# Residuals of four attention layers held by tokens, and planned tiles in place of rings, in a two-layer network on one Trainium2 core

## The chip, the cores and the metric

The kernel runs on one core of a Trainium2 chip. The core has five engines that run at the same time and wait for each other by semaphores: TensorE (PE: matmuls and transposes, results into PSUM), VectorE (DVE), ScalarE (ACT), GpSimd (POOL) and SyncE (SP, which issues DMAs here). PSUM is divided into 8 tiles of 128 x 512 floats in this kernel; POOL works on SBUF alone here. The metric is the device time in microseconds (us) of one execution. The median of three runs before the change is 562.79 us (561.96 to 564.04).

## What is computed

The input is 2048 tokens of 128 features (8 sequences of 256). Two layers follow, each with an attention part and a feed-forward part, and a normalisation `(x - mean) / sqrt(var + eps)` after each residual sum.

- First layer: a simple attention, a router, and for each token the two best of 8 expert networks.
- Second layer: two grouped convolutions over the tokens, then four layers of linear attention, a feed-forward part of width 512, and a second one with four weight matrices of width 512.

The change concerns the second layer's attention. Cut to what matters:

```
h = layernorm(conv2(gelu(conv1(x))) + x, ln0_g, ln0_b)
for i in range(4):
    q, k = gelu(h @ Wq[i] + bq[i]) + 0.21, gelu(h @ Wk[i] + bk[i]) + 0.21
    v = h @ Wv[i] + bv[i]
    z  = 1 / (q . mean(k) + 1e-6)          # per head and token
    kv = rope(k)^T v / n
    out = rope(q) kv * z
    h = layernorm(out + h, lnA_g[i], lnA_b[i])   # (t - mean) / sqrt(var) * g + b
f = gelu(h @ W1 + b1) @ W2 + b2
h = layernorm(f + h, ln2_g, ln2_b)
```

The residual of each layer, the `h` in `out + h`, is thus a normalised tile times a factor plus a shift per feature.

## The kernel before

The first layer ends near 185 us with the experts' results scattered to DRAM (`ys`). For the second layer the tokens are cut into 4 blocks of 512 (`blk`, two sequences each). `second_layer(blk)` doesn't issue instructions at once. It adds steps to a plan (`Steps.add`, by way of `do`), each with its engine, a cost in ns, the tiles it reads and writes and the new tiles it takes. `Steps.order` then makes one order for all engines by list scheduling: among the steps that could start first, with those up to 50 ns later, it picks the one with the highest rank (length of the longest chain behind it) plus a bias of its block, 3000 * (NB - blk) ns. Each engine's instructions are issued in that order and run in order on the chip, so a waiting instruction holds up all behind it on its engine. `Steps.trace` issues them.

A new tile comes from a ring: 8 PSUM tiles (`ps`), 21 tiles of 128 x 512 (`tmp`), 5 wide ones (`hid`), 7 of `featT`, 2 of `got`, 4 each of `xp` and `kvh`. A ring hands out its buffers in turn, so a step waits until the oldest one has been read for the last time.

The steps of a block, with the lines of the profile:

- SP fetches the experts' results (`got`, L882). DVE adds both to the residual, four sub-tiles with two instructions each, in one step (L890, L891), takes the moments (L823, L825), POOL makes the root (L343, and a power at L344), DVE centres and scales (L846), PE transposes (L868), ACT copies into the padded tile (L915).
- Convolutions: 20 matmuls each (L921, L938) with four GELUs between (L930), the sum (L944), transposes back to tokens, moments, root, centring into `n0`, transposes to features, and on ACT the factor and shift into `h0` (L954).
- One attention layer, with `h` by features: PE makes k (L970), q (L981) and v (L993); ACT the GELUs (L977, L982, L986); PE transposes k (L1015). DVE multiplies by the rope tables: for k from PSUM (L1018, L1024), for q from SBUF (L1035, L1033), and POOL adds the two halves (L1030 for k, L1037 for q). PE forms k^T v (L1044), DVE masks it by heads (L1050); PE forms the denominators (L1058, L1062) from means (L1005) and DVE inverts them (L1072, L1073); PE forms the numerators (L1079), DVE multiplies them by z (L1085).
- The residual: PE transposes `h` back to tokens (`back`, L1092) into a PSUM tile `pr`, and DVE adds it to the result `s` (L1095).
- The norm of the layer: DVE takes moments of `s`, POOL makes root and shift (L343, L344, L836, L837), ACT scales and shifts `s` in place (L857), PE transposes it (L868), ACT applies the layer's factor and shift by features into the next `h` (L954).
- The feed-forward parts: L1109 and L1120, then L1153, L1173 (two wide products) and L1194, the last block's in two halves; the result goes to DRAM (L1207).

The lines of the residual before:

```
def back():
    for i in range(NT):
        nc.tensor.transpose(t("pr")[:, i * P : (i + 1) * P], T(hT)[:, i * P : (i + 1) * P], ident)

do_("PE", 600, back, f"{hT} s", pr="ps")
do_("DVE", 680, lambda: nc.vector.tensor_add(t("s"), t("pr"), t("s")), "pr", "s")
```

Of the kernel before, what the change touches and what calls it, by code (L numbers as in the profile page):

```python
# [10 lines left out]
F32 = mybir.dt.float32  # L11
# [57 lines left out]
    ("bv", L * D), ("ln2_g", D), ("ln2_b", D),  # L69
# [63 lines left out]
class Steps:  # L133
# [19 lines left out]
    def order(self):  # L153
# [10 lines left out]
        over, taken, free = {}, {ring: [] for ring in self.rings}, {}  # L164
        ready, found = [i for i in range(n) if not missing[i]], []
        while ready:
            starts = {}
            for i in ready:
                engine, cost, _, needs, new, _, bias = self.steps[i]
                t = free.get(engine, 0)  # L170
                for d in needs:
                    on, lag = self.steps[d][0], self.steps[d][5]
                    t = max(t, end[d] + lag + (self.HOP.get(on, 80) if on != engine else 0))
                for name, ring in new.items():
                    at = len(taken[ring]) - self.rings[ring][0]
                    if at >= 0:
                        t = float("inf") if left[taken[ring][at]] else max(t, over[taken[ring][at]])
                if t < float("inf"):
                    starts.setdefault(engine, []).append((t, i))
            if not starts:  # L180
                raise AssertionError([(self.steps[i][0], self.steps[i][4], {r: [(x, left[x]) for x in taken[r][-self.rings[r][0]:]] for r in self.steps[i][4].values()}) for i in ready])
            first = min(min(s)[0] for s in starts.values())
            t, i = max(
                ((t, i) for s in starts.values() if min(s)[0] == first for t, i in s if t <= first + 50),
# [6 lines left out]
            for name, ring in new.items():  # L191
                taken[ring].append(name)
# [11 lines left out]
    def trace(self):  # L204
        for i in self.order():
            _, _, run, _, new, _, _ = self.steps[i]
            for name, ring in new.items():
                self.tiles[name] = self.rings[ring][1]()
            run()
# [3 lines left out]
def tile_network(ctx: ExitStack, tc: tile.TileContext, a: dict, out: bass.AP):  # L213
# [558 lines left out]
    tmpp = ctx.enter_context(tc.tile_pool(name="tmp1", bufs=21))  # L772
    pairp = ctx.enter_context(tc.tile_pool(name="pairs", bufs=2))
# [12 lines left out]
    def chunked(ap):  # L786
# [6 lines left out]

    plan = Steps({
        "ps": (8, ps), "tmp": (21, tmp), "hid": (5, hidden), "featT": (7, featT),
        "got": (2, lambda: pairp.tile([P, NT, K, D], F32, tag="got", name="got")),
        "xp": (4, lambda: tmpp.tile([P, BB, PADN], F32, tag="xp", name="xp", bufs=4)),
        "kvh": (4, lambda: tmpp.tile([P, BB, D], F32, tag="kvh", name="kvh", bufs=4)),
# [3 lines left out]
    def second_layer(blk):  # L802
# [3 lines left out]
        def do(engine, cost, run, reads="", writes="", lag=0, behind="", **new):  # L806
            plan.add(
                engine, cost, run, of(reads), of(writes) + of(" ".join(new)),
                {f"{n}.{blk}": ring for n, ring in new.items()}, lag, 3000 * (NB - blk), of(behind),
            )  # L810
# [7 lines left out]
        def moments_of(src, mv, n=NT, at=0, cost=1240):  # L818
# [9 lines left out]
            do("DVE", cost * n // NT, run, src, mv)  # L828
# [13 lines left out]
        def centre(dst, src, mv, r, n=NT, at=0, cost=1120, **new):  # L842
# [8 lines left out]
            do("DVE", cost * n // NT, run, f"{src} {mv} {r}", "" if dst in new else dst, **new)  # L851
# [12 lines left out]
        def turn(dst, src, n=NT, at=0):  # L864

            def run():
                for i in range(at, at + n):
                    nc.tensor.transpose(T(dst)[:, i * P : (i + 1) * P], T(src)[:, i * P : (i + 1) * P], ident)  # L868

            do("PE", 590 * n // NT, run, src, **{dst: "ps"})  # L870
# [8 lines left out]
        def fetch():  # L879
            for k in range(K):  # L880
                at = k * B * N + blk * TB
                nc.sync.dma_start(out=T("got")[:, :, k, :], in_=ys[at : at + TB, :].rearrange("(i p) d -> p i d", p=P))  # L882

        do("SP", 1200, fetch, lag=1800, got="got")

        def combine():
            for i in range(NT):
                n = blk * NT + i
                s, x = by_tile(T("s"))[:, i, :], xs[blk][:, i, :]
                nc.vector.scalar_tensor_tensor(s, T("got")[:, i, 0, :], m1[:, n : n + 1], x, ALU.mult, ALU.add)  # L890
                nc.vector.scalar_tensor_tensor(s, T("got")[:, i, 1, :], m2[:, n : n + 1], s, ALU.mult, ALU.add)  # L891

        do("DVE", 2300, combine, "got", s="tmp")
        if blk == 0:

            do("ACT", 1500, lambda: nc.scalar.activation(
                small.tile([P, 1], F32, tag="warm", name="warm"), T("s")[:, 0:1], AF.Gelu), "s", "")
        moments_of("s", "mvc")
        root_of("mvc", "rc", 1e-5)

        def own():
            keep_as("x", res().rearrange("p i d -> p (i d)"))

        do("DVE", 0, own, "", "x")
        centre("x", "s", "mvc", "rc")
        turn("px", "x")


        def padded():
            for t in (T("xp"), T("h1").rearrange("p (g b n) -> p g b n", g=NG, b=BB)):  # L910
                nc.vector.memset(t[..., 0:2], 0.0)
                nc.vector.memset(t[..., N + 2 : N + 4], 0.0)

        do("DVE", 200, padded, xp="xp", h1="hid")
        do("ACT", 600, lambda: nc.scalar.copy(T("xp")[:, :, 2 : N + 2], by_batch(T("px"))), "px", "xp")  # L915

        def conv1():
            for k in range(KW):
                for g in range(NG):
                    at = slice(g * CG, (g + 1) * CG)  # L920
                    nc.tensor.matmul(  # L921
                        T(f"pg{g}"), lhsT=taps1[at, k, :], rhs=T("xp")[at, :, k : k + N],
                        start=(k == 0), stop=(k == KW - 1), tile_position=(g * CG, 0),
                    )

        do("PE", 4600, conv1, "xp", **{f"pg{g}": "ps" for g in range(NG)})
        for g in range(NG):
            def gelu1(g=g):
                h1 = T("h1").rearrange("p (g b n) -> p g b n", g=NG, b=BB)
                nc.scalar.activation(h1[:, g, :, 2 : N + 2], by_batch(T(f"pg{g}")), AF.Gelu, bias=col("conv1_b", g))  # L930

            do("ACT", 640, gelu1, f"pg{g} h1", f"hg{g}")

        def conv2():
            h1 = T("h1").rearrange("p (g b n) -> p g b n", g=NG, b=BB)
# [7 lines left out]
        do("PE", 5900, conv2, "h1 hg0 hg1 hg2 hg3", pc="ps")  # L943
# [15 lines left out]
        def attention(l, hT, out):  # L959
# [130 lines left out]
            def back():  # L1090
                for i in range(NT):
                    nc.tensor.transpose(t("pr")[:, i * P : (i + 1) * P], T(hT)[:, i * P : (i + 1) * P], ident)  # L1092

            do_("PE", 600, back, f"{hT} s", pr="ps")
            do_("DVE", 680, lambda: nc.vector.tensor_add(t("s"), t("pr"), t("s")), "pr", "s")  # L1095
# [12 lines left out]
        for c in range(FC):  # L1108
# [9 lines left out]
            by_tile(T("xb")), by_tile(T("x")), row("ln2_b").unsqueeze(1).to_broadcast([P, NT, D])), f"x {hT}", xb="tmp")  # L1118
# [100 lines left out]
def _laid_out(v):  # L1219
# [6 lines left out]
    def by_group(x):  # L1226
# [24 lines left out]
        "ln2_g": v["L1_attn_ln2_g"], "ln2_b": v["L1_attn_ln2_b"],  # L1251
    }
# [38 lines left out]
```

## Time and profile before

| what | value |
|---|---|
| median of three runs | 562.79 us |
| the profiled execution's own time | 559.73 us |
| its span, first to last instruction | 558.0 us |
| mean granted TensorE clock | 0.935 |
| first layer's last result written to DRAM | 187.3 us |
| first transpose of the second layer (L868) | 197.4 us |
| first product of an attention layer (L970) | 242.2 us |
| first L1109 (feed-forward) | 358.9 us |
| last product of an attention layer (L1079) | about 366 us |
| end of the last L1194 | 547.4 us |
| transposes back, L1092 | 64, 9.7 us busy |

The profile records one execution. "Busy" is the time in which an engine had at least one instruction under way; since instructions overlap in an engine's pipeline, and matmuls above all, a mean duration is longer than the distance from one start to the next. A group's line gives line, engine, operation, output and input tiles, shapes and count, then busy us and mean ns of one, then the idle time of the engine just before them and what ended it. A window's line gives the stretch and its length, then busy us and number of instructions of PE, PEld (weight loads), DVE, ACT and POOL, then the granted clock, the DMA share and GB/s. A wait's line gives who waited for whom, us in all, times, and the longest. fp32 matmuls count as two passes, transposes as one.

### The profile page before, as it was taken

Reading aid. Unit: us, or ns where it says so; the run is one execution under the profiler, and the core shown is the slowest. Engines: PE = TensorE matmul, PEld = TensorE weight load, DVE = VectorE, ACT = ScalarE, POOL = GpSimd, SP = SyncE. Lnnn points to the kernel's source line nnn. Section 1 sums busy time; section 2 is a strip of 40 time slices with the busy share of each in tenths; the row PEclk is TensorE's granted clock in tenths of the full one; section 3 lists DMA queues with packets and bytes.
Section 4 is the critical chain, followed back from the end, with each engine's and each line's share of the span. In section 5 each row is a group of like instructions: output and inputs, shape, how many; then the busy total and the mean of one; then the engine's idle time right before and its main releaser. Section 6 shows DMA issues by size and latency. Waiting matters only on the chain.

```text
span 558.0 us, 7642 instructions
## 1 busy us (share of the span) xinstructions
PE 494.5 (89%) x2557; PEld 332.5 (60%) x2557; DVE 299.7 (54%) x1009; ACT 221.6 (40%) x478; POOL 202.0 (36%) x275
## 2 busy tenths in 40 slices
PE   5875289999999079999999899999999999999992
PEld 3655179999999033467787778754444444444442
DVE  1996524444444491379999999938943020022232
ACT  4561044444444123163958676654322120312110
POOL 1860375777643220035565555644200000000011
PEclk9965569999999679999999999999999999999997
DMA  7950476776661320000000000000000000000001
GB/s 250 351 177 1 137 237 217 232 241 216 203 217 70 108 64 1 2 1 1 1 2 0 2 2 1 1 1 1 0 1 1 0 1 0 1 0 1 19 23 34
DMA packets 22727, 39.27 MB, mean 70 GB/s; under 512 B 2880, under 2 KB 15936, under 8 KB 22560
## 3 DMA queue, kind: packets, MB, share of 16 engines
q1 hardware_dynamic: 19600, 33.40, 18.2%
q0 software_dynamic: 2496, 5.12, 2.8%
q8 instruction: 20, 0.33, 0.2%
q10 hardware_dynamic: 592, 0.27, 0.2%
q14 instruction: 19, 0.16, 0.1%
HBM read 34.12 MB, written 4.65 MB: 69 GB/s over the span
## 4 chain that ended last, share of the span: by engine, by line
PE 66%; DVE 10%; POOL 7%; issue 5%; DMA 3%; ACT 2%; POOLq 0%; DVEq 0%; SPq 0%
PE ps L1173 20%; PE ps L720 9%; PE ps L1153 5%; PE ps L733 4%; PE ps L921 4%; PE ps L938 3%; PE ps L1109 3%; PE ps L1194 2%; PE ps L1120 2%; POOL ys L744 2%; PE ps L868 2%; DMA xg<-x,source 2%; PE ps L1079 2%; POOL root L344 2%; PE ps L970 2%
## 5 line engine op out<-in xcount | busy, mean ns | idle before, releaser
L343 POOL TENSOR_SCALAR root<-mv 128x4 f32<-128x4 f32 (+1 forms) x45 | 11.0, 245 | 227.4 <-DVE mv L825 220.2
L720 PE MATMUL ps<-xT,hid 128*128 128x256 f32 (+1 forms) x368 | 74.6, 358 | 0.0
L726 DVE SCALAR_TENSOR_TENSOR gate<-ps,hid,gl 128x256 f32<-128x256 f32 (+1 forms) x92 | 40.7, 444 | 54.4 <-ACT gl L725 52.7
L720 PEld LDWEIGHTS ps<-xT,hid 128*128 128x128 f32 x368 | 63.2, 200 | 6.2
L1173 PE MATMUL ps<-hid,gh 128*128 128x512 f32 x128 | 58.5, 592 | 0.0
L1173 PE MATMUL ps<-tmp,gh 128*128 128x512 f32 x128 | 58.2, 592 | 0.0
L344 POOL TENSOR_TENSOR root<-root,minus_half 128x4 f32<-128x4 f32 (+1 forms) x53 | 55.2, 1042 | 4.4
L725 ACT ACTIVATE gl<-ps,hid 128x256 f32<-128x256 f32 (+1 forms) x92 | 40.5, 442 | 32.8 <-PE ps L720 29.2
L744 POOL DMA_INDIRECT ys<-y,dest x39 | 38.4, 984 | 26.5 <-DVE y L739 16.8
L700 POOL DMA_INDIRECT xg<-x,source x39 | 37.8, 969 | 26.4 <-PE ps L709 9.8
L1158 DVE SCALAR_TENSOR_TENSOR tmp<-tmp,ps 128x512 f32<-128x512 f32 x16 | 10.9, 682 | 64.1 <-ACT tmp L1156 64.1
L1173 PEld LDWEIGHTS ps<-hid,gh 128*128 128x128 f32 x128 | 24.2, 190 | 29.7 <-issue 28.7
L1173 PEld LDWEIGHTS ps<-tmp,gh 128*128 128x128 f32 x128 | 24.2, 190 | 29.7 <-issue 29.7
L733 PE MATMUL ps<-hid,gate 128*128 128x128 f32 x312 | 38.4, 275 | 0.0
L733 PEld LDWEIGHTS ps<-hid,gate 128*128 128x128 f32 x312 | 37.8, 192 | 0.8
L857 ACT ACTIVATE tmp<-tmp,shift,root 128x128 f32<-128x128 f32 x64 | 26.3, 483 | 12.0 <-POOL shift L837 11.9
L1153 PE MATMUL ps<-featT,g 128*128 128x512 f32 x64 | 30.9, 592 | 0.0
L1178 ACT ACTIVATE tmp<-ps,cols 128x512 f32<-128x512 f32 x16 | 11.0, 687 | 47.9 <-PE ps L1173 47.8
L1030 POOL TENSOR_TENSOR tmp<-tmp 128x512 f32<-128x512 f32 x16 | 20.3, 1268 | 21.1 <-DVE tmp L1018 10.3
L1178 ACT ACTIVATE hid<-ps,cols 128x512 f32<-128x512 f32 x16 | 11.0, 687 | 42.2 <-PE ps L1173 42.1
L986 ACT ACTIVATE tmp<-ps,cols 64x512 f32<-64x512 f32 x32 | 21.9, 683 | 13.1 <-PE ps L981 12.7
L711 ACT COPY xT<-ps 128x256 f32<-128x256 f32 (+1 forms) x23 | 7.8, 340 | 46.6 <-PE ps L709 46.6
(185 smaller groups left out, 917.3 us busy)
## 6 DMA issues: line engine op xcount, KB each, us to landing
hid<-in_experts_dram SPq DMA_DIRECT2D x23, 836.0 KB, 4.8
got<-ys SPq DMA_DIRECT2D x8, 256.0 KB, 2.9
counts<-in_counts_dram SPq DMA_DIRECT2D x1, 1032.0 KB
featT<-in_xT_dram SPq DMA_DIRECT2D x4, 256.0 KB, 4.2
res<-in_x_dram SPq DMA_DIRECT2D x4, 256.0 KB, 5.1
gh<-in_h1T_dram SPq DMA_DIRECT2D x1, 1024.0 KB, 7.5
gh<-in_h2T_dram SPq DMA_DIRECT2D x1, 1024.0 KB
x<-res SPq DMA_DIRECT2D x4, 256.0 KB, 2.3
```

What stands on the lines that cost most here:

```text
L344: nc.gpsimd.tensor_tensor(r, r, minus_half[:, :n], ALU.pow)
L700: landed[t] = nc.gpsimd.indirect_dma_start(out=rows_in[t][:, j, :], out_offset=None, in_=x1, in_offset=bass.IndirectOffsetOnAxis(ap=source ...
L720: keep(nc.tensor.matmul(p[:, half * m : (half + 1) * m], lhsT=part(t, "w1", half * F + c * P, P), rhs=xT, start=True, stop=True,))
L725: keep(nc.scalar.activation(gl, p[:, m : 2 * m], AF.Gelu_apprx_tanh, bias=part(t, "b1", FC + c, 1)))
L726: keep(nc.vector.scalar_tensor_tensor(g[:, c, :m], p[:, :m], part(t, "b1", c, 1), gl, ALU.add, ALU.mult))
L733: keep(nc.tensor.matmul(p[:, j * D : (j + 1) * D], lhsT=g[:, c, j * P : (j + 1) * P], rhs=part(t, "w2", c * D, D), start=(c == 0), stop=(c ...
L744: put = nc.gpsimd.indirect_dma_start(out=ys, out_offset=bass.IndirectOffsetOnAxis(ap=dest[:, u : u + 1], axis=0), in_=y[:, j, :], in_offse ...
L857: nc.scalar.activation(by_tile(T(dst))[:, i, :], by_tile(T(src))[:, i, :], AF.Identity, bias=T(sh)[:, i : i + 1], scale=T(r)[:, i : i + 1],)
L921: nc.tensor.matmul(T(f"pg{g}"), lhsT=taps1[at, k, :], rhs=T("xp")[at, :, k : k + N], start=(k == 0), stop=(k == KW - 1), tile_position=(g ...
L1153: do("PE", 853, lambda p=p, w=w, c=c: nc.tensor.matmul(T(f"{p}{c}"), lhsT=w[:, c * P : (c + 1) * P], rhs=T("xT"), start=True, stop=True), ...
L1173: do("PE", 853, lambda c=c, i=i, w=w, dst=dst, src=src: nc.tensor.matmul(T(f"p{dst}{c}"), lhsT=w[:, i, c * P : (c + 1) * P], rhs=chunk(src ...
L1178: do("ACT", 690, lambda c=c, dst=dst, scale=scale: nc.scalar.activation(chunk(dst, c), T(f"p{dst}{c}"), AF.Gelu, scale=col(scale, c)), f"p ...
```

## The change

Four things change in the second layer; the first layer's code is the same.

1. **The residual by tokens.** The transposes back (L1092) are gone. In their place POOL multiplies the normalised tile, which is already by tokens (`n0`, or the previous layer's `s`), by the factor and then adds the shift, both as rows spread over all partitions, in place, once PE has transposed that tile (`pn`). DVE then adds this SBUF tile to `s`. The rows `ln0_g`, `ln0_b`, `lnA_g` and `lnA_b` (three layers) are loaded with the other rows: 1792 floats per partition, where there were 768.
2. **A stock in place of rings.** All tiles of the second layer are made ahead and kept. A step takes whichever tile of its kind has been free longest by the plan, not the next in turn.
3. **The planner's choices.** Among the steps that could start first it no longer takes in those up to 50 ns later, and the blocks' biases are 0, -8000, -13000 and -16000 in place of steps of 3000.
4. **The start of a block.** The sum of the experts' results is four steps, one per sub-tile, in place of one. A division into parts is written in, but `parts` is 1 for every block, so fetch, transposes, copy and convolution are whole as before.

The core of the diff:

```diff
-    ("bv", L * D), ("ln2_g", D), ("ln2_b", D),
+    ("bv", L * D), ("ln2_g", D), ("ln2_b", D), ("ln0_gr", D), ("ln0_br", D), ("lnA_gr", (L - 1) * D), ("lnA_br", (L - 1) * D),
...
+        def since(name):
+
+            return 0 if name is None else float("inf") if left[name] else over[name]
...
-                for name, ring in new.items():
-                    at = len(taken[ring]) - self.rings[ring][0]
-                    if at >= 0:
-                        t = float("inf") if left[taken[ring][at]] else max(t, over[taken[ring][at]])
+                for ring in set(new.values()):
+                    t = max(t, sorted(map(since, held[ring]))[list(new.values()).count(ring) - 1])
...
-                ((t, i) for s in starts.values() if min(s)[0] == first for t, i in s if t <= first + 50),
+                ((t, i) for s in starts.values() if min(s)[0] == first for t, i in s if t <= first + 0),
...
-                taken[ring].append(name)
+                had = held[ring]
+                at = min(range(len(had)), key=lambda k: since(had[k]))
+                had[at], self.place[name] = name, at
...
-                self.tiles[name] = self.rings[ring][1]()
+                self.tiles[name] = self.rings[ring][self.place[name]]
...
-                {f"{n}.{blk}": ring for n, ring in new.items()}, lag, 3000 * (NB - blk), of(behind),
+                {f"{n}.{blk}": ring for n, ring in new.items()}, lag, (0, -8000, -13000, -16000)[blk], of(behind),
...
-        do("DVE", 2300, combine, "got", s="tmp")
...
+            for i in range(h * n, (h + 1) * n):
+                def combine(i=i):
+                    at = blk * NT + i
+                    s, x = by_tile(T("s"))[:, i, :], xs[blk][:, i, :]
+                    nc.vector.scalar_tensor_tensor(s, T("got")[:, i, 0, :], m1[:, at : at + 1], x, ALU.mult, ALU.add)
+                    nc.vector.scalar_tensor_tensor(s, T("got")[:, i, 1, :], m2[:, at : at + 1], s, ALU.mult, ALU.add)
+
+                do("DVE", 600, combine, f"got got{h}" + (" s" if i else ""), f"s_{h}", **({} if i else {"s": "tmp"}))
...
-            do_("PE", 600, back, f"{hT} s", pr="ps")
-            do_("DVE", 680, lambda: nc.vector.tensor_add(t("s"), t("pr"), t("s")), "pr", "s")
...
+                n = f"s{l - 1}" if l else "n0"
+                g, b = ("lnA_gr", l - 1) if l else ("ln0_gr", 0), ("lnA_br", l - 1) if l else ("ln0_br", 0)
+                for which, op, done in ((g, ALU.mult, "tg"), (b, ALU.add, "tb")):
+                    do("POOL", 1270, lambda which=which, op=op: nc.gpsimd.tensor_tensor(
+                        by_tile(T(n)), by_tile(T(n)), row(*which, D).unsqueeze(1).to_broadcast([P, NT, D]), op
+                    ), f"{n} pn{l}" + (f" tg{l}" if done == "tb" else ""), f"{done}{l}")
+                do("DVE", 680, lambda: nc.vector.tensor_add(t("s"), T(n), t("s")), f"{n} tb{l}", f"s{l}")
```

The lines move. In the changed kernel L992, L1003 and L1015 are the products k, q and v; L1037 the transposes of k; L1040 and L1046, L1055 and L1057 the rope products of DVE; L1052 and L1059 POOL's rope sums for k and q; L1027 the means; L1101 the numerators; L1107 and L1120 the product with z and the residual add; L1117 POOL's factor and shift; L1141, L1152 and L1155 the first feed-forward part and its sum.

## Prediction

> **What bounds the kernel now.** I read, in this order, the busy shares, the windows of the second part, the waits of PE, the timeline and the groups by form. The page first:
>
> ```profile
> span 558.0 us, 7642 instructions
> PE 494.5 (89%) x2557; PEld 332.5 (60%) x2557; DVE 299.7 (54%) x1009; ACT 221.6 (40%) x478; POOL 202.0 (36%) x275
> ```
>
> Over the whole run PE leads and POOL is two thirds idle. That is an average over stages, so the windows come next (stretch and length; busy us of PE, PEld, DVE, ACT, POOL; clock):
>
> ```profile
> 280.00:300.00 20.00, 19.56 (x136) 15.90 (x136) 19.67 (x63) 12.99 (x32) 12.61 (x19) 1.00 0.00 1
> 320.00:340.00 20.00, 19.29 (x135) 15.67 (x136) 19.15 (x57) 14.99 (x35) 11.42 (x16) 1.00 0.00 1
> ...
> 420.00:440.00 20.00, 20.00 (x48) 8.89 (x47) 3.75 (x6) 4.12 (x6) 0.00 (x0) 1.00 0.00 0
> ```
>
> From 243 to 362 us the attention layers run: PE and VectorE (DVE) both look full, GpSimd (POOL) has 8 of 20 us free. After that PE alone is full. PE's waits are small, behind that for the first transpose:
>
> ```profile
> PE ps L868 <- DVE res L846: 14.7, 1, 14.7
> PE ps L1044 <- POOL tmp L1030: 2.3, 3, 1.0
> ```
>
> But a busy PE is pipelined, so I count its work by the distance between starts:
>
> ```profile
> 295.52 0.60 PE L868 MATMUL ps<-ident,tmp 128*128 128x128 f32 x4
> 295.96 0.60 PE L1092 MATMUL ps<-ident,featT 128*128 128x128 f32 x4
> 296.39 1.06 PE L993 MATMUL ps<-wv,featT 128*128 128x128 f32 x8
> ```
>
> Four transposes last 0.60 but the next group starts 0.44 later: 0.11 a pass. A 512-column pass is 0.43 (8.58 us for 20 of L1173 in the chain). So counted, PE has 39.3 us of work in the convolutions (197.4 to 242.2: 44.8 us), 117.1 from the first L970 to block 0's last L1120 (242.2 to 370.0: 127.9) and 176.9 from there to the last L1194 (547.4: 177.3). The last stretch is PE's alone. In the middle one PE lacks 10.8 us. DVE there: start-to-start times (0.60 for 512 elements, 0.20 a stats, 0.08 an aggregate and so on) times the counts give 104.1 us from the first L1005 to the last step at 362.2, and with the 9.2 us of holds below 113.3 of 117.8: 96%. So DVE, not PE, sets the pace of the attention stage, with PE close behind.
>
> **What the change removes.** L1092, four transposes per layer and block, 64 in all:
>
> ```profile
> L1092 PE MATMUL ps<-ident,featT 128*128 128x128 f32 x64 | 9.7, 274 | 0.0
> L1095 DVE TENSOR_TENSOR tmp<-ps,tmp 128x512 f32<-128x512 f32 x16 | 10.7, 672 | 0.0
> L1037 POOL TENSOR_TENSOR tmp<-tmp 128x512 f32<-128x512 f32 x16 | 20.3, 1270 | 15.3 <-DVE tmp L1033 10.5 <-PE ps L1044 3.9 <-DVE means L1005 0.7
> L1033 DVE SCALAR_TENSOR_TENSOR tmp<-tmp,tabs 128x512 f32<-128x512 f32 x16 | 11.7, 729 | 0.0
> L1035 DVE SCALAR_TENSOR_TENSOR tmp<-tmp,tabs 128x512 f32<-128x512 f32 x16 | 15.4, 965 | 0.0
> ```
>
> 64 x 0.11 = 7.0 us leave PE (9.7 if the row's busy time were the price). One PSUM tile per layer is no longer taken.
>
> **What it adds on POOL.** 32 tensor_tensor of 128x512 (factor, then shift); the nearest rows are L1037 and L1030, 1.27 us: 40.6 us. A layer now gives POOL two rope sums (2.54), a root (0.24 + 1.04) and a shift (0.5), 4.3 us of the 7.52 that a layer takes (the L344 rows at 317.64 and 347.72 are four layers apart). It becomes 6.9: it fits, barely. The factor waits for PE's transposes of its tile; behind it in POOL's queue stand roots and rope sums of other blocks, each up to 2.5 us later. A block's own chain through a layer is about 17 us by the rows, a round of four layers 30, so that lateness has room: zero, and at most the 2.5 us once.
>
> **What it does to DVE.** The add stays, but reads two SBUF tiles in place of PSUM and SBUF. Undisturbed that costs the same (0.68, the shortest L1033). Yet such an instruction meets POOL:
>
> ```profile
> 282.25 1.27 POOL L1030 TENSOR_TENSOR tmp<-tmp 128x512 f32<-128x512 f32 x1
> 283.11 0.96 DVE L1035 SCALAR_TENSOR_TENSOR tmp<-tmp,tabs 128x512 f32<-128x512 f32 x1
> ...
> 289.71 1.04 POOL L344 TENSOR_TENSOR root<-root,minus_half 128x4 f32<-128x4 f32 x1
> 290.23 0.68 DVE L1035 SCALAR_TENSOR_TENSOR tmp<-tmp,tabs 128x512 f32<-128x512 f32 x1
> ```
>
> POOL's sum ends at 283.52; L1035, started under it, ends 0.55 later: it stood still until POOL was done. I went through all 48 starts of DVE instructions with two SBUF inputs here (L1033, L1035 and the small L1005): 14 fell into one of POOL's 1.27 us sums, each was held to its end, 9.2 us in all, 0.19 per start, with POOL in such a sum 34% of the time (40.6 of 118.5 us). L1095, with a PSUM input, was never held.
>
> A rule that speaks against the change stands in the Trainium skill, SBUF — State Buffer, section "Who interferes with whom": a DVE instruction with two SBUF inputs and a GpSimd instruction that reads SBUF exclude each other, and the first keeps the ports for its whole length. For the sums the rows agree. For the roots they don't: the second L1035 above ran at full speed under a power of 1.04 us. So I count only the four sums: 5.08 of about 8.1 us per layer, 63% in place of 34%, 0.19 x 63/34 = 0.355 us per start. By the rule, with roots and shifts (some 87%), 0.49.
>
> **Sum of the attention stage.** The built program puts 103.2 us of undisturbed DVE work between the first L1027 (means) and block 0's L1155 (104.7 in before), with 59 two-input starts: 59 x 0.355 = 20.9. At the 96% of before that is 124.1 / 0.96 = 129.3, plus 2.2 from the first L992 to the first means (242.2 to 244.4 in before): 131.5. PE's work from the first L992 to block 0's last L1152 is 112.2, with block 3's two convolutions (9 us) moved into the stretch and some of the later blocks' layers moved behind it. PE lacks 131.5 - 112.2 = 19.3 us, in place of 10.8: +8.5 against the 7.0 removed.
>
> **The order and the stock.** The wider spacing of priorities changes the start. Block 1's combine is split by tile, so block 0's centre starts after three tiles of it, some 0.6 us earlier (root ready at 195.95, centre at 196.91). Against that, block 0's second convolution now stands ahead of block 1's first and waits for four GELUs, 0.61 apart from 205.33 on: 1.4 us of idle PE where before had 0.7. Together +0.1. After the last L1194 the instructions are the same. A tile of the stock waits for its last readers as one of a ring does; no wait of before names such a release above 0.2 us: zero, between -1 and +1. The larger row table (7 KB per partition in place of 3, 0.5 MB) loads in the first 40 us; at slice 2's 351 GB/s that is 1.5 us, ahead of a slice with 1 GB/s, and its first use is near 240 us: nothing; 1.5 us without that gap. SP's fetches of got stay in order.
>
> **Sum.** -7.0 + 8.5 + 0.1 = +1.6 us. The profiled execution took 559.73 us (span 558.0); the median of the three runs is 562.79, 3.1 above. I add the difference to the median: 564.4.
>
> **Rivals.**
>
> *POOL's sums fall where DVE doesn't ask.* At the old 0.19 per start DVE's stretch is 2.2 + (103.2 + 11.3) / 0.96 = 121.5, PE lacks 9.3, and -7.0 - 1.5 + 0.1 = -8.4: 554.4. For it: two of the four sums wait for DVE results and so follow its two-input work. Against it: factors and shifts wait only for PE.
>
> *Lockstep.* Where POOL always has a next sum, it takes the ports when DVE lets go. Walking one layer from the end of k's product: rope sum 0.1 to 1.37, the residual add held 0.8; factor 1.95 to 3.2, the next product held 0.65; shift to 5.1, the second product held 1.25; means held 0.3: 3.0 per layer, 0.75 per start. Half way from 0.355 is 0.55: 32.5 us of holds, stretch 143.6, net +13.7: 576.5. By the skill's rule, 0.49, it is +9.9: 572.7. The sign turns at 0.33 per start (19.4 us), close to my value.
>
> *Nothing happens*: PE's saving becomes idle time one for one, 562.8.
>
> **How the numbers follow.** My case, 0.28 to 0.43 per start, reaches from 560 to 569 and has 0.42. Within 0.5% (2.8 us, about what a measurement tells from no change) lies 0.26 of it (up to 0.375 per start), above 0.16. The first rival has 0.34, all faster; lockstep 0.22, all slower; nothing happens 0.02. Faster 0.34, same 0.28, slower 0.38. The range runs from just below the first rival to lockstep, 553 to 577.
>
> **What would show it.** L1117 x32 at 1.27 us, POOL near 17 of 20 us in the attention windows; L1055, L1057 and L1120 at means of 0.9 to 1.1 us where 0.68 is undisturbed; block 0's L1155 some 131 us after the first L992; PE full afterwards. It is wrong if these rows stay near 0.75, if PE idles in the later layers, or if roots come so late that DVE itself waits.

## The result and the profile after

The changed kernel took 578.51 us (median of four runs, 576.01 to 579.49), the kernel before 562.38 us beside it: 1.0273 of it (95% interval 1.0240 to 1.0307). On another chip it was 1.0323 (1.0291 to 1.0355). The forecast was 564.4 us, its range ended at 577. So the change loses 15 to 19 us where I had 1.6.

The profiled execution took 576.01 us. Its page, span and busy shares:

```profile
span 574.2 us, 7526 instructions
...
PE 495.7 (86%) x2493; PEld 329.1 (57%) x2493; DVE 319.9 (56%) x1009; ACT 222.4 (39%) x478; POOL 250.8 (44%) x307
```

PE's busy time is that of before (494.5 us), though 9.7 us of transposes are gone from it, in a longer span. DVE has 20 us more with the same 1009 instructions, POOL 49 us more. The windows of the same places (stretch; PE, PEld, DVE, ACT, POOL; clock):

```profile
280.00:300.00 20.00, 16.45 (x106) 12.56 (x106) 19.49 (x44) 13.79 (x34) 18.72 (x22) 1.00 0.00 0
...
320.00:340.00 20.00, 17.45 (x103) 13.43 (x104) 19.62 (x46) 12.90 (x31) 16.59 (x21) 0.91 0.00 1
...
420.00:440.00 20.00, 20.00 (x51) 9.13 (x50) 1.69 (x4) 5.29 (x8) 0.00 (x0) 1.00 0.00 0
```

In these two windows of the attention layers POOL has 16.6 and 18.7 of 20 us, DVE is full as before, and PE has lost 2 to 3 of 20 us. Afterwards PE is alone and full, as it was. Between 320 and 340 us the granted clock is 0.91, which the kernel before shows nowhere in this stage. PE's waits, with the first transpose for comparison:

```profile
PE ps L878 <- DVE res L856: 14.5, 1, 14.5
PE ps L1080 <- DVE means L1027: 12.6, 10, 2.4
...
PE ps L1066 <- POOL t L1052: 4.2, 5, 1.7
```

New is the wait of the denominators (L1080) for the small means (L1027), ten times. The groups of POOL's sums and DVE's instructions with two SBUF inputs (busy us, mean ns):

```profile
L1117 POOL TENSOR_TENSOR t<-t,rows 128x512 f32<-128x512 f32 x32 | 47.4, 1482 | 10.2 <-PE ps L878 9.5
...
L1052 POOL TENSOR_TENSOR t<-t,t 128x512 f32<-128x512 f32 x16 | 22.8, 1424 | 0.1
...
L1055 DVE SCALAR_TENSOR_TENSOR t<-t,tabs 128x512 f32<-128x512 f32 x16 | 19.5, 1218 | 0.0
...
L1057 DVE SCALAR_TENSOR_TENSOR t<-t,tabs 128x512 f32<-128x512 f32 x16 | 18.7, 1167 | 0.0
...
L1120 DVE TENSOR_TENSOR t<-t,t 128x512 f32<-128x512 f32 x16 | 15.8, 988 | 1.3 <-DVE t L1107 0.5
...
L1027 DVE SCALAR_TENSOR_TENSOR means<-ksum,tabs 128x32 f32<-128x32 f32 x16 | 8.4, 526 | 1.2 <-ACT t L999 1.2
```

Undisturbed, L1055, L1057 and L1120 take 0.68 us and L1027 0.18, so the stage lost 16 x (0.54 + 0.49 + 0.31 + 0.35) = 27 us in 64 starts, 0.42 per start. Before it was 9.2 us in 48, 3.9 of it on the means:

```profile
L1005 DVE SCALAR_TENSOR_TENSOR means<-ksum,tabs 128x32 f32<-128x32 f32 x16 | 6.7, 426 | 1.3 <-ACT tmp L977 1.3
```

Counted in the timelines, 47 of the 59 starts in the stretch fall under a sum of POOL, whose sums fill 65% of it; before it was 15 of 48, at 33% (14 of them held, as the prediction counted). POOL is held too: its factor and shift last 1.48 us where 1.27 is undisturbed. The timeline shows how:

```profile
314.13 1.11 DVE L1120 TENSOR_TENSOR t<-t,t 128x512 f32<-128x512 f32 x1
...
314.65 1.72 POOL L1052 TENSOR_TENSOR t<-t,t 128x512 f32<-128x512 f32 x1
...
315.76 1.16 DVE L1057 SCALAR_TENSOR_TENSOR t<-t,tabs 128x512 f32<-128x512 f32 x1
...
316.33 1.72 POOL L1117 TENSOR_TENSOR t<-t,rows 128x512 f32<-128x512 f32 x1
...
316.84 1.75 DVE L1055 SCALAR_TENSOR_TENSOR t<-t,tabs 128x512 f32<-128x512 f32 x1
```

Each waits for the one above it on the other engine. L1120 keeps the ports until 315.2, so POOL's L1052 takes 0.45 us longer; that one ends at 316.37, and L1057, started under it, half a microsecond later; POOL's next sum waits for L1057 and ends at 318.05, and L1055 stands from 316.84 until then. DVE spends 1.75 us on 0.68 us of work.

By stages, from the traces (us):

| kernel | first transpose to first k product | from there to block 0's sum L1155 (before: L1123) | to the last L1226 (before: L1194) | all three |
|---|---|---|---|---|
| before | 44.8 | 127.9 | 176.9 | 349.6 |
| after, predicted | | 131.5 | | 351.2 |
| after | 35.3 | 143.7 | 186.4 | 365.4 |

The first and the third together are 221.7 us in both kernels: block 3's convolutions have moved from the first into the middle, work of the later blocks from the middle into the third. The whole loss is in the middle. Against the forecast, 12.2 us were missed in the middle and 2.0 outside it (351.2 - 131.5 = 219.7 was forecast there).

### The profile page after: what moved, and what is told of

Same layout as the page of the kernel before. It is cut to its first block, busy times and chain, and to the rows that moved or that the text cites. A ratio compares the mean times of both kernels' runs of the same rounds, so it can differ in the third digit from the quotient of the medians.

```text
span 574.2 us, 7526 instructions
## 1 busy us (share of the span) xinstructions
PE 495.7 (86%) x2493; PEld 329.1 (57%) x2493; DVE 319.9 (56%) x1009; ACT 222.4 (39%) x478; POOL 250.8 (44%) x307
## 4 chain that ended last, share of the span: by engine, by line
PE 54%; DVE 26%; issue 6%; POOL 5%; DMA 2%; ACT 0%; POOLq 0%; DVEq 0%; SPq 0%
PE ps L1205 19%; PE ps L727 8%; PE ps L1185 5%; PE ps L740 4%; PE ps L942 4%; DVE t L1055 3%; PE ps L960 3%; DVE stats L833 3%; DVE t L1057 2%; PE ps L1226 2%; POOL ys L751 2%; DVE t L1120 2%; PE ps L1152 2%; DVE t L1107 2%; DMA xg<-x,source 2%
## 5 line engine op out<-in xcount | busy, mean ns | idle before, releaser
L1205 PE MATMUL ps<-t,gh 128*128 128x512 f32 x128 | 58.7, 592 | 0.0
L1117 POOL TENSOR_TENSOR t<-t,rows 128x512 f32<-128x512 f32 x32 | 47.4, 1482 | 10.2 <-PE ps L878 9.5
L1190 DVE SCALAR_TENSOR_TENSOR t<-t,ps 128x512 f32<-128x512 f32 x16 | 11.0, 686 | 60.1 <-ACT t L1188 60.1
L1205 PEld LDWEIGHTS ps<-t,gh 128*128 128x128 f32 x128 | 24.1, 190 | 29.2 <-issue 28.9
L867 ACT ACTIVATE t<-t,shift,root 128x128 f32<-128x128 f32 x64 | 26.3, 482 | 23.4 <-POOL shift L847 23.4
L833 DVE BATCH_NORM_STATS2 stats<-ps 128x6 f32<-128x128 f32 x48 | 10.7, 283 | 33.4 <-PE ps L878 33.4
L1188 ACT ACTIVATE t<-ps,half 128x512 f32<-128x512 f32 x16 | 11.0, 686 | 38.4 <-PE ps L1185 38.3
```

What stands on the lines that cost most here:

```text
L833: nc.vector.bn_stats(stats[:, i, :], by_tile(T(src))[:, at + i, :])
L867: nc.scalar.activation(by_tile(T(dst))[:, i, :], by_tile(T(src))[:, i, :], AF.Identity, bias=T(sh)[:, i : i + 1], scale=T(r)[:, i : i + 1],)
L1117: do("POOL", 1270, lambda which=which, op=op: nc.gpsimd.tensor_tensor(by_tile(T(n)), by_tile(T(n)), row(*which, D).unsqueeze(1).to_broadca ...
L1205: do("PE", 853, lambda c=c, i=i, w=w, dst=dst, src=src: nc.tensor.matmul(T(f"p{dst}{c}"), lhsT=w[:, i, c * P : (c + 1) * P], rhs=chunk(src ...
```

## The experiments

The kernels were measured on several chips, each time beside the kernel before, whose median was 561 to 568 us by the chip (the first layer's part differs). Between chips only ratios are compared; 1% is 5.6 us. "Stretch" is the middle column above. "Holds" are summed as above, over the DVE instructions with two SBUF inputs: 9.2 us in the kernel before, 26.8 in the changed one. Theory H: DVE's instructions with two SBUF inputs and POOL's sums hold each other. Q: POOL is late because it is full. O: the new order and the stock cost.

**e1_back**: the changed kernel with the transposes back in all layers.

```diff
-            if (blk, l) in ((0, 0), (0, 1), ...
+            if (blk, l) in ():
```

> The changed kernel with the residual by PE's transposes again in every layer (the branch that the change leaves in place); stock, planner's numbers and split combine stay. Theory H, POOL's sums hold DVE's two-input instructions: the loss goes, 556 to 565 us. Rival O, the new order and stock cost the time: it stays near 574 to 580. Rival Q, POOL's fuller queue makes roots late: as H here, 556 to 565.

1.0072 (1.0042 to 1.0103), stretch 135.1, holds 9.9 us. Most of the loss and nearly all of the new holds go; order and stock cost something by themselves, which I had at +0.1 us.

**e2_pow** and **e3_none**: POOL's 32 sums replaced by powers on a tile of 5 columns, of nearly the same length, or left out; in both the residual lacks factor and shift.

```diff
-  nc.gpsimd.tensor_tensor(by_tile(T(n)), by_tile(T(n)), row(*which, D)..., op)
+  nc.gpsimd.tensor_tensor(five, ones[:, :5], T(n)[:, :5], ALU.pow)      # e2
+  None                                                                  # e3
```

> The changed kernel in the same order on every engine, but each of POOL's 32 factor and shift instructions is a power of 128x5 elements with about the same duration (0.71 us for 2 elements and 1.04 for 4 give 1.2 for 5), reading only 5 columns; factor and shift of the residual are left out. H: DVE's holds fall from 27 us to about 12 and the run to 560 to 567 us. Q: POOL is as busy and as late as before, so it stays at 574 to 579. O: 574 to 579.

> The changed kernel in the same order on every engine, with the 32 factor and shift instructions left out altogether (so factor and shift of the residual are not applied). H: like the power version, 558 to 566 us, the two within 3 us. Q: the power version stays slow and this one is fast, 558 to 566. O: 574 to 579.

e2: 1.0033 (1.0015 to 1.0052), stretch 129.9. e3: 0.9991 (0.9971 to 1.0012), stretch 127.4. The groups of e2:

```profile
L1117 POOL TENSOR_TENSOR five<-ones,t 128x5 f32<-128x5 f32 x32 | 42.5, 1339 | 0.7 <-DVE t L856 0.7
...
L1120 DVE TENSOR_TENSOR t<-t,t 128x512 f32<-128x512 f32 x16 | 15.3, 957 | 0.5
...
L1057 DVE SCALAR_TENSOR_TENSOR t<-t,tabs 128x512 f32<-128x512 f32 x16 | 14.0, 874 | 0.0
...
L1055 DVE SCALAR_TENSOR_TENSOR t<-t,tabs 128x512 f32<-128x512 f32 x16 | 11.9, 747 | 0.0
```

POOL's 32 instructions are there, 42.5 us of them, in the same order, and POOL's windows have 17.4 to 19.6 of 20 us. But the two rope products fall from 1.2 to 0.75 and 0.87 us, the holds from 26.8 to 12.0 us as expected, and 2.4% of the 2.7% loss is gone (2.9% of 3.2% by the other chip). So a full POOL costs 0.4% (e2 over e3), the holding of the ports 2.4 to 2.9%. Two other things change with the edit. The powers write a tile of their own, so POOL no longer waits for PE's transposes (9.5 us before L1117) nor DVE's add for POOL; but that add waited 1.3 us in all. And PE's clock no longer falls, which can be 3.4 us of it (last section). For the powers the prediction's row was right against the page's rule: in e2's timeline 31 of DVE's two-input instructions start under a power, and none of them is held.

**e4_order**: the changed kernel with the planner's old numbers.

```diff
-  ... (0, -8000, -13000, -16000)[blk] ...      t <= first + 0
+  ... 3000 * (NB - blk) ...                    t <= first + 50
```

> The changed kernel with the old planner's numbers (biases 3000 apart, steps up to 50 ns later taken in); residual by tokens and stock stay. H: still slow, 572 to 582 us. O: most of the loss goes, 561 to 567. Q: 572 to 582.

1.0390 (1.0334 to 1.0446), stretch 149.0. The new order is not the cause of the loss; beside the holds (27.7 us here) it is the better one, by 0.7 to 1.2%.

**e7_stock** and **e8_numbers** split e1's loss: e1 with the old numbers (the stock and the split sum of the experts' results are left), and the kernel before with the new numbers.

> The changed kernel with the transposes back in every layer (e1) and with the old numbers of the planner as well (biases 3000 apart, starts up to 50 ns later taken in): against the kernel before only the stock of tiles and the split combine are left. Stock as the cause of the 4 us that e1 lost: 565 to 567. Numbers as the cause: 560.5 to 562.5. Both together: between.

> The kernel before, with its rings, its whole combine and its transposes back, and only the planner's new numbers (biases 0, -8000, -13000, -16000 and no 50 ns). Numbers as the cause of the 4 us that e1 lost: 564 to 567. Stock as the cause: 560.5 to 562.5. A ring that hands out tiles in turn may suit the new spacing worse than a stock does: then above 568.

e7: 1.0026 (1.0008 to 1.0045). e8: 1.0112 (1.0089 to 1.0136), stretch 135.8. Of e1's 0.7% the numbers are 0.5 and the rest 0.3. In e1 DVE's busy time in the stretch is that of before (115.5 us), so more is not done; PE and DVE both have gaps:

```profile
320.00:340.00 20.00, 18.81 (x118) 14.59 (x119) 17.99 (x55) 12.44 (x30) 12.56 (x17) 0.94 0.00 1
```

**e5_inplace**: the product by z written in place into its PSUM tile, so that the residual add reads PSUM and SBUF.

```diff
-  t("s")..., t("po")..., t("z")...), "po z", s="tmp")
+  t("po")..., t("po")..., t("z")...), "po z", "po")
-  nc.vector.tensor_add(t("s"), T(n), t("s"))
+  nc.vector.tensor_add(t("s"), t("po"), T(n))
```

> The changed kernel with the product by z (L1107) written in place into its PSUM tile, so that the residual add (L1120) reads PSUM and SBUF, as the add of the kernel before did; POOL's factor and shift stay. H (DVE instructions with two SBUF inputs stand still under POOL's sums): the add can't be held any more; in block 0's stretch it lost 16 x (0.99 - 0.68) = 4.9 us, so some 573.5 us (570 to 575.5), L1120 at a mean below 0.75, L1055 and L1057 still near 1.2. Where POOL's sums merely move their holds over to L1055 and L1057: 577 to 579, with those two above 1.3. Q (POOL's lateness) and O (order): no change, 577 to 580.

1.0163 (1.0118 to 1.0208), stretch 140.4; the add's mean is 0.69, L1055 still has 1.22. With one instruction per layer off the ports, and none of POOL's work changed, 6 to 9 us of the 15 to 19 go, somewhat more than the 4.9 counted; the holds fell from 26.8 to 20.0. The four executions took 574.5 to 580.8 us, and the profiled one is of the slower (580.4), so the gain is clear in sign and uncertain in size.

**e6_pieces**: factor and shift in four instructions of 128x128 each.

> The changed kernel with POOL's factor and shift (L1117) each in four instructions of 128x128 in place of one of 128x512; the rope sums stay whole. H, and each POOL instruction gives the ports back at its end: DVE waits for a piece of about a third of a microsecond rather than for up to 1.27 us, so holds by factor and shift fall to a third: of the 15.6 us of holds some 6 come back, 572 us (569 to 575), L1055, L1057 and L1120 at means near 1.0. H, but POOL takes the ports again for the next piece at once: 577 to 582. Q: POOL's four starts take longer than one, so POOL is later still: 579 to 584.

1.0345 (1.0313 to 1.0376). A piece takes 0.457 us (columns: min/median/max ns), so four take 1.83 in place of 1.27, and POOL is completely full:

```profile
L1119 POOL TENSOR_TENSOR t<-t,rows x128: 444/457/1028, 235.4 to 386.8; 128x128 f32<-128x128 f32 x128
```

```profile
320.00:340.00 20.00, 15.02 (x98) 11.72 (x98) 16.78 (x45) 12.46 (x29) 19.67 (x36) 1.00 0.00 1
```

L1055 and L1057 fell to 0.94 and 0.92 us: holds do get shorter with the instruction that holds. Holds are 13.2 us in all. But PE now waits for POOL's rope sums, 17 us in all:

```profile
PE ps L1066 <- POOL t L1052: 8.6, 7, 1.9
PE ps L1101 <- POOL t L1059: 8.6, 6, 3.2
```

So here it is Q's cause that sets the time. The plan still prices the four pieces at the 1.27 us of one; what an order made with their true price would give was not tried. In this order shorter holds for a longer POOL are a bad trade.

**e9_free** and **e16_free_psum**: old numbers, no transposes back, factor and shift left out; e16 adds e5's edit.

> The changed kernel with the old numbers of the planner and with POOL's factor and shift left out (the residual added is the normalised tile without them), so no transposes back and no cost for what takes their place: what the change could have won at best in the old order. If the 7.0 us of transposes are worth their time on PE: 0.987 to 0.991 of the kernel before. If DVE sets the pace of the stretch whatever PE has to do: 0.995 to 1.004, with PE idle for some 7 us more in block 0's stretch.

> e9 (old numbers, no transposes back, POOL's factor and shift left out) with the product by z in place in PSUM, so that the residual add reads PSUM. It is open why e9, with 7.0 us less for PE and nothing in their place, was no faster. H: its add read two SBUF tiles and was held by the rope sums alone, 16 x (1.18 - 0.68) = 8.0 us: with that gone 0.987 (0.983 to 0.992). If DVE's own work sets the pace whatever is held: 0.996 to 1.002.

e9: 0.9990 (0.9974 to 1.0007). e16: 0.9859 (0.9826 to 0.9891), stretch 120.8. The add in e9 and in e16:

```profile
L1118 DVE TENSOR_TENSOR t<-t,t 128x512 f32<-128x512 f32 x16 | 18.9, 1183 | 0.6
...
L1055 DVE SCALAR_TENSOR_TENSOR t<-t,tabs 128x512 f32<-128x512 f32 x16 | 10.9, 682 | 0.0
```

```profile
L1118 DVE TENSOR_TENSOR t<-ps,t 128x512 f32<-128x512 f32 x16 | 11.1, 692 | 0.8
```

This is the plainest pair. With no new sum on POOL at all, 13 of the 16 adds from two SBUF tiles start under one of the rope sums that were always there, and lose 8.0 us together. L1055 in the same kernel stands at 0.68, undisturbed: it never starts under a sum now. So a part of the holds has only moved, and in all they are 12.0 us against 9.0 in e7 and 3.3 in e16; that eats nearly the whole worth of the transposes. With the add on PSUM the kernel gains 1.4%.

**e15_add_old**: e4 with e5's edit. **e11_tokens_psum**: that, and q's cosine product reads PSUM: ScalarE activates q a second time in place, and the sine product comes first. **e10_psum**: q's edit alone, in the kernel before.

```diff
+  do_("ACT", 680, lambda: nc.scalar.activation(t("pq"), t("pq"), AF.Gelu, bias=col("bq", l)), "pq q qx", "pq")
...
-  by_batch(t("qr")), by_batch(t("q")), SHIFT, cosT, ...
+  by_batch(t("qr")), by_batch(t("pq")), SHIFT, cosT, ...
```

> The changed kernel with the old numbers of the planner and only the product by z in place in PSUM: e11 without its part for q. e4 lost 3.9% and e11 nothing, and it is open which of the two parts gave that back. Holds that add up one by one: the add had 16 x (1.09 - 0.68) = 6.5 us in e4, so 1.028 (1.024 to 1.032), the rest being q's. If it is the alternation of POOL and DVE that costs, and breaking it once per layer is enough: 1.005 to 1.018.

> The changed kernel with the old numbers of the planner, the product by z in place in PSUM (as in e5) and q's rope products as in e10: of DVE's two-input instructions only the sine product and the small means read two SBUF tiles. H: with two of three large ones out of reach, holds in the stretch fall from 27 to some 10 us; e4 stood at 1.039, so some 16 us less: 1.010 (1.002 to 1.020). If POOL's sums then hold the sine product and the means all the longer, or POOL being full sets the pace: 1.022 to 1.035.

> The kernel before with q's rope products changed: ScalarE writes the activated q a second time, in place into its PSUM tile (16 activations of some 0.69 us more), the sine product comes first and the cosine product then reads that PSUM tile. One instruction with two SBUF inputs fewer per layer, and the one left comes before POOL's sum for k can start. H: of the 9.2 us of holds in the attention stage the sine product's 4.5 go, DVE sets the pace there, so 0.992 to 0.996 of the kernel before, the two products at 0.68 to 0.75. If PE sets the pace or ScalarE's extra work and the longer life of the PSUM tile come in: 0.999 to 1.010.

e15: 1.0174 (1.0129 to 1.0220). e11: 1.0001 (0.9983 to 1.0020), stretch 127.5. e10: 1.0165 (1.0140 to 1.0191). e15 gives back 12 us where the add's holds were 6.5, and so falls just into the range of the second reading. The means were held less as well (0.68 to 0.53 us, 2.4 us in all), what DVE saves is worth somewhat more than itself where DVE is at 91% of the stretch, and PE has 10 us less at half its clock (last section); these were not parted, so that it is the alternation is not shown. In e11 DVE's busy time in the stretch is 18.7 us less than in e4 (117.6 for 136.3), the stretch 21.5 us shorter: holds and time go together (9.3 us of holds for 27.7), though PE's half clock goes with them. e10 is a miss. Its groups, sine, cosine, means:

```profile
L1034 DVE SCALAR_TENSOR_TENSOR tmp<-tmp,tabs 128x512 f32<-128x512 f32 x16 | 15.5, 970 | 0.0
...
L1036 DVE SCALAR_TENSOR_TENSOR tmp<-ps,tabs 128x512 f32<-128x512 f32 x16 | 11.0, 684 | 0.1
...
L1006 DVE SCALAR_TENSOR_TENSOR means<-ksum,tabs 128x32 f32<-128x32 f32 x16 | 9.2, 573 | 2.8 <-ACT tmp L977 2.8
```

The hold did not vanish, it moved to whichever product still reads SBUF (0.97), and the means got worse (0.57; 0.43 before). Holds are 11.0 us in all, 1.8 more than before, which is far from the loss. PE waited 9.6 us for DVE's sum for v, 2.0 before. Why it lost as much as 1.6% stays open.

**after_again**: the changed kernel once more, beside these.

> The changed kernel itself, on the chip of this call, beside which the other three are read: 1.024 to 1.031 of the kernel before if the loss doesn't depend on the chip. e5 stood at 1.016 on another chip; if this run is below 1.020, the gain of e5 is not shown.

1.0323 (1.0291 to 1.0355): the loss doesn't hang on one chip.

**e13_both_psum**: e11 with ScalarE's exchanged copy of q in a PSUM tile too.

```diff
-  do_("ACT", 1340, gelu_qx, "pq", qx="tmp")
+  do_("ACT", 1340, gelu_qx, "pq", qx="ps")
```

> e11 with ScalarE's second copy of q (halves exchanged) put into a PSUM tile of its own in place of an SBUF tile, so that the sine product reads PSUM too: of DVE's two-input instructions only the small means still read two SBUF tiles, while POOL does all four sums of a layer. H: e11 had 16 x (0.99 - 0.68) = 5.0 us of holds left on the sine product and DVE sets the pace: 0.991 (0.986 to 0.996) of the kernel before, faster than both kernels, with POOL still near 19 of 20 us. If POOL being full sets the pace: 0.998 to 1.003. If the PSUM tile more per layer runs short: above 1.003.

0.9893 (0.9862 to 0.9924), 560.83 us beside 567.20, stretch 121.3: faster than both kernels, with all of POOL's new work in it.

```profile
300.00:320.00 20.00, 19.62 (x139) 15.91 (x138) 19.61 (x61) 15.99 (x38) 19.50 (x24) 1.00 0.01 1
320.00:340.00 20.00, 19.79 (x141) 16.27 (x140) 19.61 (x57) 18.54 (x42) 19.42 (x25) 1.00 0.01 2
```

```profile
L1118 POOL TENSOR_TENSOR t<-t,rows 128x512 f32<-128x512 f32 x32 | 40.7, 1273 | 6.2 <-PE ps L878 5.8
...
L1121 DVE TENSOR_TENSOR t<-ps,t 128x512 f32<-128x512 f32 x16 | 11.1, 692 | 1.1
...
L1058 DVE SCALAR_TENSOR_TENSOR t<-ps,tabs 128x512 f32<-128x512 f32 x16 | 10.9, 681 | 0.1
...
L1056 DVE SCALAR_TENSOR_TENSOR t<-ps,tabs 128x512 f32<-128x512 f32 x16 | 10.4, 648 | 0.0
...
L1028 DVE SCALAR_TENSOR_TENSOR means<-ksum,tabs 128x32 f32<-128x32 f32 x16 | 7.0, 435 | 1.6 <-ACT t L999 1.6
```

POOL has 19.5 of 20 us in these windows (87% of the stretch), and hardly anything is late for it: PE is back at 19.6 and more, and the longest of its waits for POOL is 0.8 us. All large products stand at 0.65 to 0.69 us, POOL's sums at 1.27. Only the small means are still held, 4.1 us in all.

**e14_means**: e13 with the means made from one SBUF tile and a factor per partition.

```diff
-  nc.vector.scalar_tensor_tensor(means, t("ksum")..., SHIFT * N, tab("head")..., ALU.add, ALU.mult)
+  nc.vector.tensor_scalar_add(t("ksum"), t("ksum"), SHIFT * N)
+  for b in range(BB):
+      nc.vector.tensor_scalar(means[:, b, :], tab("head"), t("ksum")[:, b : b + 1], None, ALU.mult)
```

> e13 with the means made by three small instructions with one SBUF tile each (an add of the constant, and for each sequence the table times a factor per partition) in place of one with two. H: no DVE instruction of the attention layers can be held; the means lost 16 x (0.43 - 0.18) = 4.0 us in e11 and the three cost some 1.5 us more of DVE: 0.3 to 0.5% below e13, and no wait of PE's denominators for the means above 1 us in all. If the instruction with a factor per partition counts as one with two SBUF inputs: as e13 or above.

1.0378 (1.0351 to 1.0404), the largest miss: 4.9% above e13. The two small instructions (min/median/max ns), and two of them in the timeline:

```profile
L1030 DVE TENSOR_SCALAR means<-tabs,ksum x32: 220/1190/1327, 251.1 to 389.4; 128x16 f32<-128x16 f32 x32
```

```profile
284.12 2.53 DVE L1030 TENSOR_SCALAR means<-tabs,ksum 128x16 f32<-128x16 f32 x2
284.13 1.26 POOL L1117 TENSOR_TENSOR t<-t,rows 128x512 f32<-128x512 f32 x1
...
285.35 1.26 POOL L1059 TENSOR_TENSOR t<-t,t 128x512 f32<-128x512 f32 x1
```

A product of 16 columns takes 0.22 us free and 1.19 in the median: each of the two waits for a whole sum of POOL. POOL starts its next sum at 285.35 as the first of them gets its turn, and the second waits for that. PE's denominators wait for them:

```profile
PE ps L1080 <- DVE means L1030: 17.6, 13, 2.4
```

**e17_back_psum** (e7 with q's two products from PSUM, transposes back) and **e18_new_psum** (e13 with the new numbers).

> e13 with the transposes back in place of the residual by tokens: stock, old numbers, q's two products from PSUM, the add from PSUM as in the kernel before, and no factor and shift on POOL. It tells what the change itself is worth once nothing of DVE is held: e13 less this run. H: it has the stretch free of holds but 7.0 us more for PE, which by e13 is the bound of the stretch (19.4 to 19.8 of 20 us): 1.000 to 1.004 of the kernel before, 1.1 to 1.4% above e13. If the PSUM tile more for pr beside the one for q's copy runs short: 1.005 to 1.02. If e13's gain is all from q's products and none from the residual: 0.989.

> e13 with the planner's new numbers. O (the new numbers cost some 4 to 6 us whatever else is done, as in e8 and e1): 0.998 to 1.000. If they cost only where DVE is held, or were found for the residual by tokens and suit it: 0.985 to 0.991.

e17: 0.9953 (0.9938 to 0.9968). e18: 0.9941 (0.9915 to 0.9967). So where nothing large is held, the residual by tokens is worth 0.6% (e13 over e17), half of the 7.0 us that PE saves, and the new numbers cost 0.5% (e18 over e13; the two intervals touch). e17 was itself better than I expected: q's products from PSUM pay without the change too.

## Why the prediction was wrong

The sign of each of its two main terms was right, the balance was not. Going along its own steps:

**Transposes, -7.0 us.** Right in sign; the size depends on what stands beside it: e7 to e16 is -1.7% (9 us, with 5.7 us fewer holds in it), e1 to e3 -0.8% (4.5 us, with the holds of a two-SBUF add in it), e17 to e13 -0.6% (3.4 us, with POOL's new sums).

**The hold per start: the step that failed first.** "63% in place of 34%, 0.19 x 63/34 = 0.355 us per start". Measured 0.42 in 64 starts. The step treats DVE's starts as falling on POOL's sums at random, by the share of time. That share came out as forecast (65% of the stretch for 63%), and in the kernel before and in e9, with two sums per layer, the starts do fall so: 15 of 48 and 19 of 64, at 33 and 32%, and e9's holds are 0.19 per start (12.0 us in 64). In the changed kernel, with four, they do not: 47 of 59 starts fall under one. A hold delays POOL's sum, which then meets DVE's next one (the timeline above); the two engines fall into step. On 59 starts the miss is 0.065 x 59 = 3.8 us of DVE.

**"At the 96% of before": the second failure, and the larger one.** The 96% was DVE's share from the first means to 362.2 us. The step divides by it the work up to L1155, which in the kernel before comes at 370.1: put through the same step, the kernel before gets (104.7 + 9.2) / 0.96 + 2.2 = 120.8 us, where its stretch has 127.9. The share that belongs to this stretch is 113.9 / 127.9 = 89%. With it and the predicted holds the stretch is 124.1 / 0.89 = 139.4, 7.9 us more; with the measured 0.42 it is (103.2 + 24.8) / 0.89 = 143.8, 4.4 us more, and 143.7 was measured. Putting the kernel before through the sum would have shown it. That the last sum comes so close is in part luck: the share isn't fixed (e1, with DVE work as before, has the stretch of 135.1 us, a share of 84%), and the sum has no term for the new numbers or for PE's clock.

**The order and the stock, +0.1 (between -1 and +1).** The stock, with the split sum, is +1.5 us (e7). The numbers cost 2.6 us more with the transposes back (e1 over e7), 6.3 us with the rings (e8), 2.7 us without holds (e18 over e13). I had looked at the start of the stage alone. In e1 DVE does the work of before (115.5 us) in a longer stretch, at 85%: it is not DVE that sets the pace there. With the holds, DVE is back at 91% and sets it again, and then the new order is 4 to 7 us better than the old (e4). So its cost and that of the holds don't add.

**POOL's lateness, zero, at most 2.5 us.** 2.4 us with powers in place of sums (e2 over e3); within the bound, and the fear of a full POOL was wrong: e13.

**The rule and the row.** That powers don't hold DVE stood up (e2, at 1.34 us each). The rule's 0.49 per start is as far above the measured 0.42 as my 0.355 is below it; its time of 572.7 us came nearer than mine only because the share of 96% made both too small.

**Rivals.** Lockstep named a stretch of 143.6 and 576.5 us, and its picture, the engines taking turns, is what the timeline shows. Its number is right by luck: 0.55 per start at a share of 96%, where 0.42 at 89% was measured. The first rival falls: POOL's sums do meet DVE's. Nothing is left of "nothing happens".

Summed up with the new numbers: stock +1.5, numbers +2.6, transposes out and the add on two SBUF tiles -4.6, POOL's time +2.4, the holds by its sums +13.5 (2.4% of 562, PE's clock included): +15.4 us. These are the steps from the kernel before through e7, e1, e3 and e2 to the changed kernel, so they must add up to the 15.4 measured; the size of each depends on the path, as e4 shows. What stays open: where in the order e8 and e1 lose, and e10.

## What to carry to other kernels

Before an elementwise step is moved between engines, look at where its operands lie: an add with one input in PSUM was never held by GpSimd's sums, the same add from two SBUF tiles lost half a microsecond on average to sums that were there all along. Two engines that hold each other are not priced by the average share of time once one of them always has a next instruction; walk the queue order of both, for a hold delays the other engine into the next one. Here the cure was neither to take the work away nor to cut it up, but to leave intermediate results in PSUM (e13), and then a GpSimd busy for 87% of the stretch made hardly anything late.

## What the runs showed of the hardware beside this

**One small SBUF tile can be enough.** In e14 a DVE tensor_scalar of 128x16 with one SBUF tile and a factor per partition waited for whole sums of POOL (0.22 us free, 1.19 in the median), as did, at times, the add of a constant to 128x2 (up to 1.28 us). The Trainium skill, SBUF — State Buffer, section "Who interferes with whom", says that tensor_scalar from SBUF to SBUF can run in a mode that takes both pairs of ports and so contends with GpSimd; e14's waits fit that, at 16 columns too; which mode the instructions ran in, no run here shows.

**PE's granted clock falls to half in spells of 3.4 us.** In the attention layers it is 1.00 in the kernel before and in all runs with a stretch under 129 us; in the longer stretches it falls in some windows. e4 (columns as above, the clock is the third from the end):

```profile
260.00:280.00 20.00, 17.10 (x90) 14.08 (x91) 18.38 (x47) 11.96 (x27) 15.11 (x19) 0.83 0.00 1
280.00:300.00 20.00, 16.73 (x121) 13.94 (x120) 19.24 (x45) 12.70 (x31) 19.27 (x19) 1.00 0.00 1
...
320.00:340.00 20.00, 16.31 (x102) 13.12 (x103) 19.32 (x51) 10.65 (x24) 16.48 (x19) 0.91 0.00 1
```

Narrower windows show what these means are made of. The changed kernel, one spell with the 3.4 us ahead of it:

```profile
318.98:322.40 3.42, 2.36 (x19) 2.31 (x20) 3.38 (x15) 0.90 (x3) 3.25 (x6) 1.00 0.00 0
322.40:325.80 3.40, 3.40 (x13) 2.47 (x12) 3.16 (x4) 2.06 (x7) 3.32 (x3) 0.50 0.02 5
```

One such spell within 20 us gives 0.915, two give 0.83. The busy share of a wide window doesn't decide: in e6 PE had 15.0 of 20 us busy between 320 and 340 at 1.00. The Trainium skill, TensorE: Matmul & The Clock Gate, Part 1, says that the clock is at half after an idle window of some 3.4 us. The length agrees; but here PE was busy for 2.36 of the 3.42 us ahead of the spell, so it need not have been idle throughout.

A part of the loss is this second effect of the same stalls. The stretch of the changed kernel has two spells in its first profile, which is at most 3.4 us of PE's time, and seven on the other chip. There the holds (26.4 us for 26.8) and DVE's busy time (130.4 for 130.6) are the same and the stretch is 147.0 us in place of 143.7. Of the four executions of the changed kernel, too, the one at a mean clock of 0.935 took 576.0 us, those at 0.919 to 0.924 took 578.2 to 579.5.
